# Moving the loads of x, of small tables and of the shared expert at the passage from the woven layers to the mixture

## Chip, cores, metric

One of the eight cores of a Trainium2 chip. The metric is the device time of one execution in microseconds. The kernel reads and writes HBM (device memory); the host only lays arrays out ahead of the launch. In what follows PE is TensorE (matrix products and transposes), DVE is VectorE, ACT is ScalarE, POOL is GpSimd, and SP is SyncE, whose queue issues most of the transfers.

## What is computed

Two layers run on x of 16 samples, each with 256 tokens of width 256, in float32. The first three blocks (two attentions and a quantized feed-forward, with their conditioning) come first; the change lies at the start of the fourth line below.

```python
x = x + attn0(cross_attention(x, fside, braak_embed, itok_B_0_5))
x = x + ffn0(x @ cat_w[itok_B_0_63] + cat_b[itok_B_0_63])
x = x + attn1(diffuse(x, zX, zY, zR))
x = x + ffn1(cond2(x, itok_B_0_15))

def cond2(x, indices):                     # one set of "own" weights for each sample
    h = gelu(x @ fc1_w.T + fc1_b)          # 256 -> 1024, exact gelu
    shared = h @ fc2_w.T + fc2_b           # 1024 -> 192
    own = h @ experts_w[indices].T + experts_b[indices]   # 1024 -> 64
    return concatenate([shared, own], -1)

def ffn1(y):                               # 8 experts, best two, and a shared one
    gates = best_two(softmax(y @ w_router.T))
    acc = gelu(y @ Ws1.T + bs1) @ Ws2.T + bs2
    for e in range(8):
        acc += gates[:, e] * (gelu(y @ W1[e].T + b1[e]) @ W2[e].T + b2[e])
    return acc / sqrt(1.25)
```

## The kernel before

The program has two parts. `woven` runs the first three blocks: nine generators, one for each stage, are merged by a planner with a cost for each instruction, and the order is then written out as it stands. At the end of a sample, its x is written to an HBM tensor of its own, `xd[b]` (L951; shown as L160 by the profile, since the planner records all instructions on that line). The last such write is that of sample 15.

`mixture` (L1034) runs the rest. Its instructions are written in plain order, and a scheduler puts them in order on each engine by what it thinks is ready; each engine then executes its own list in order. SP's list matters here. A transfer issued by SP signals one of eight semaphores, taken in turn, and where a later transfer takes the same semaphore SP first waits until the earlier one has landed. Memory that was used by the woven part comes free with its last users, so that the first load into the tile `xs` waits for the write of `xd[15]`.

`mixture` does this, in source order:

- It loads x of all 16 samples into `xs` (L1046), 256 KiB each.
- It loads small tables: `b1` (L1052), `bs2` (L1053, scaled on DVE by L1054), and in `routing_state` the table `tri` (L1203).
- It loads the shared expert's two matrices, `w1s` and `w2s` (L1058, L1059), 1 MiB each.
- `conditioned` (L1338) loads `fc1` (1 MiB), `fc1b`, `fc2` (the array fc2a, 512 KiB), `fc2b`, `wr` (the router's weights), `expb` (the bias of the own weights, 16x64), and `shared_b`, all by a helper at L1348 or at L1357. It also loads the common part of the own weights (the array fc2c, L1370) into three buffers `own0` to `own2`, which take turns.
- `conditioned` then handles blocks of two samples (512 tokens). For each of the two it loads that sample's own weights (L1377), 128 rows of eight pieces of 256 B. It transposes the block's x on PE (L107, copies at L113 on ACT and DVE into `g_xT`), adds `bs2` to `xs` on POOL (L1387), makes the products with `fc1` (L49, gelu on ACT, L1392), with `fc2` and with `own`, and then transposes the result, multiplies it by the router's weights in the same products with `wr`, and calls `route`. `route` ranks the two best experts, with products of `r_sel` and `seen` on PE, and POOL scatters the rows to the experts' regions in HBM.
- The product of `onehot` with `expb` (L1365) gives a bias for every sample. It stands once, ahead of the blocks.
- After the eight blocks `plan_tiles` assigns expert tiles, four blocks of the shared expert follow (`shared_block`), then the expert tiles, then the other four shared blocks, with the gathering of each token's two rows (`combine`).

Here and in the profile, a line L49 is the helper `mm` for products, and L107 and L113 are the helper `transposed`.

Of the kernel before, what the change touches and what calls it, by code (L numbers as in the profile page):

```python
# [19 lines left out]
P = 128  # L20
# [24 lines left out]
def mm(nc, out, pairs, start=True, stop=True):  # L45

    last = len(pairs) - 1
    for i, (lhsT, rhs) in enumerate(pairs):
        nc.tensor.matmul(out, lhsT, rhs, start=start and i == 0, stop=stop and i == last)  # L49


def bank(k):

    return k.ps.tile([P, 512], F32, name=f"bank{k.stream}", tag=f"bank{k.stream}")


def copies(k):

    k.turn = not k.turn
    return k.nc.scalar.copy if k.turn else k.nc.vector.tensor_copy  # L60
# [973 lines left out]
def mixture(k, out):  # L1034

    nc, tc, a = k.nc, k.tc, k.a
    B, NT = k.B, 2 * k.B
    with ExitStack() as ctx:  # L1040
        k.ps = ctx.enter_context(tc.tile_pool(name="ps", bufs=4, space=bass.MemoryType.PSUM))
        keep = ctx.enter_context(tc.tile_pool(name="moe_keep", bufs=1))

        k.xs = keep.tile([P, NT, D], F32, name="xs")
        for b in range(B):
            nc.sync.dma_start(out=k.xs[:, 2 * b : 2 * b + 2, :], in_=k.xd[b].rearrange("(s p) d -> p s d", p=P))  # L1046
        k.hp = ctx.enter_context(tc.tile_pool(name="moe_h", bufs=2))
        k.p2 = ctx.enter_context(tc.tile_pool(name="moe_p2", bufs=2))
        k.yT = keep.tile([P, 2, B * S], F32, name="yT")
        k.b1 = keep.tile([P, NE + 1, 8], F32, name="b1")  # L1050
        k.bs2 = keep.tile([P, D], F32, name="bs2")
        nc.sync.dma_start(out=k.b1, in_=a["b1"])  # L1052
        nc.sync.dma_start(out=k.bs2, in_=a["b2"][NE : NE + 1].to_broadcast([P, D]))  # L1053
        nc.vector.tensor_scalar(k.bs2, k.bs2, OUT_SCALE, None, ALU.mult)  # L1054
        r = routing_state(k, keep)
        w1s = keep.tile([P, 2, FF1], F32, name="w1s")
        w2s = keep.tile([P, 8, D], F32, name="w2s")
        nc.sync.dma_start(out=w1s, in_=a["w1"][NE])  # L1058
        nc.sync.dma_start(out=w2s, in_=a["w2"][NE])  # L1059
        conditioned(k, keep, r)  # L1060
        k.stream = 1
        plan_tiles(k, keep, r)

        ew = ctx.enter_context(tc.tile_pool(name="moe_w", bufs=2))
        early = 4
        for blk in range(early):
            k.stream = blk % 2
            shared_block(k, r, w1s, w2s, blk)
        expert_tiles(k, ew, r, range(k.n_tiles - SPARE))

        used = nc.values_load(r.used[0:1, 0:1], min_val=0, max_val=k.n_tiles)
        with tc.If(used > k.n_tiles - SPARE):
            expert_tiles(k, ew, r, range(k.n_tiles - SPARE, k.n_tiles))
        for blk in range(early, NT // 4):

            for t in range(4 * (blk - early), 4 * (blk - early) + 4):
                combine(k, r, t, out)
            k.stream = blk % 2
            shared_block(k, r, w1s, w2s, blk)
            for t in range(4 * blk, 4 * blk + 4):  # L1080
                combine(k, r, t, out)


def shared_block(k, r, w1, w2, blk):
# [71 lines left out]
def combine(k, r, t, out):  # L1156

    nc = k.nc
    x = k.xs[:, t, :]
    for i in range(TOPK):  # L1160
        g = k.p2.tile([P, D], F32, name="got", tag="got", bufs=4)
        nc.gpsimd.indirect_dma_start(  # L1162
            out=g,
            out_offset=None,
            in_=k.osort[:, :],
            in_offset=bass.IndirectOffsetOnAxis(ap=r.pos_o[:, i, t : t + 1], axis=0),
        )
        nc.vector.scalar_tensor_tensor(x, g, r.gate[:, i, t : t + 1], x, ALU.mult, ALU.add)  # L1168
    nc.sync.dma_start(out=out[t // 2, (t % 2) * P : (t % 2 + 1) * P, :], in_=x)
# [168 lines left out]
def conditioned(k, keep, r):  # L1338

    nc, tc, a = k.nc, k.tc, k.a  # L1340
    B, NT = k.B, 2 * k.B
    with ExitStack() as ctx:
        w = ctx.enter_context(tc.tile_pool(name="c2_w", bufs=1))
        p2 = ctx.enter_context(tc.tile_pool(name="c2_p2", bufs=2))

        def load(name, shape, src):
            t = w.tile(shape, F32, name=name)
            nc.sync.dma_start(out=t, in_=src)  # L1348
            return t

        fc1 = load("fc1", [P, 2, FF1], a["fc1"])
        fc1b = load("fc1b", [P, 8], a["fc1b"])
        fc2 = load("fc2", [P, 8, P], a["fc2a"])
        fc2b = load("fc2b", [P, 1], a["fc2_b"][0:P].unsqueeze(1))

        wr = w.tile([P, 2, P + NE], F32, name="wr")
        nc.sync.dma_start(out=wr[:, :, P:], in_=a["w_router"])  # L1357
        nc.vector.tensor_copy(wr[:, :, 0:P], k.ident.unsqueeze(1).to_broadcast([P, 2, P]))
        expb = load("expb", [16, 64], a["L1_cond2_experts_b"])

        bias2 = w.tile([P, B], F32, name="bias2")
        shared_b = load("shared_b", [64, 1], a["fc2_b"][P : P + 64].unsqueeze(1))
        nc.vector.tensor_copy(bias2[0:64, :], shared_b.to_broadcast([64, B]))
        pb = bank(k)
        mm(nc, pb[64:128, :B], [(expb, k.onehot[0:16, 2, :])])  # L1365
        nc.vector.tensor_copy(bias2[64:128, :], pb[64:128, :B])
        own = []
        for i in range(3):
            t = w.tile([P, 8, P], F32, name=f"own{i}")
            nc.sync.dma_start(out=t[:, :, 0:64], in_=a["fc2c"])  # L1370
            own.append(t)

        for blk in range(NT // 4):
            k.stream = blk % 2
            for b in (2 * blk, 2 * blk + 1):
                which = nc.sync.value_load(k.idx[0:1, 2, b : b + 1], min_val=0, max_val=15)
                nc.sync.dma_start(  # L1377
                    out=own[b % 3][:, :, 64:128], in_=a["exp_w"][bass.ds(which, 1)].rearrange("e p f m -> p (e f) m")
                )
            xT = p2.tile([P, 2, 512], F32, name="g_xT", tag="g_xT")  # L1380
            transposed(
                k,
                xT.rearrange("p c (s t) -> p (c s) t", t=P),
                [k.xs[:, 4 * blk + s, c * P : (c + 1) * P] for c in range(2) for s in range(4)],
            )
            x = k.xs[:, 4 * blk : 4 * blk + 4, :]
            nc.gpsimd.tensor_tensor(x, x, k.bs2.unsqueeze(1).to_broadcast([P, 4, D]), ALU.add)  # L1387
            hT = k.hp.tile([P, 8, 512], F32, name="hT", tag="hT")
            for f in range(8):
                ph = bank(k)  # L1390
                mm(nc, ph, [(fc1[:, c, f * P : (f + 1) * P], xT[:, c, :]) for c in range(2)])
                nc.scalar.activation(hT[:, f, :], ph, AF.Gelu, bias=fc1b[:, f : f + 1])  # L1392
            py = bank(k)
            mm(nc, py, [(fc2[:, f, :], hT[:, f, :]) for f in range(8)])
            nc.vector.tensor_scalar(k.yT[:, 0, blk * 512 : (blk + 1) * 512], py, fc2b, None, ALU.add)
            for i in range(2):
                b = 2 * blk + i
                py = bank(k)[:, :S]
                mm(nc, py, [(own[b % 3][:, f, :], hT[:, f, i * S : (i + 1) * S]) for f in range(8)])
                nc.vector.tensor_scalar(k.yT[:, 1, b * S : (b + 1) * S], py, bias2[:, b : b + 1], None, ALU.add)  # L1400

            logits = p2.tile([P, 4, NE], F32, name="logits", tag="logits")
            part = p2.tile([P, 4, NE], F32, name="part", tag="part")
            ys = []
            for t4 in range(4):
                tok = slice(blk * 512 + t4 * P, blk * 512 + (t4 + 1) * P)
                py = bank(k)[:, : 2 * (P + NE)].rearrange("p (c w) -> p c w", c=2)
                for c in range(2):
                    mm(nc, py[:, c, :], [(k.yT[:, c, tok], wr[:, c, :])])
                nc.vector.tensor_copy(part[:, t4, :], py[:, 1, P:])  # L1410
                nc.vector.tensor_tensor(logits[:, t4, :], py[:, 0, P:], part[:, t4, :], ALU.add)
                y = p2.tile([P, 2, P], F32, name="r_y", tag="r_y", bufs=5)
                copies(k)(y, py[:, :, 0:P])
                ys.append(y.rearrange("p c d -> p (c d)"))
            route(k, r, p2, logits, ys, 4 * blk, 4)
# [105 lines left out]
```

## Time and profile before

| | |
|---|---|
| median of three runs | 2903.49 us |
| lowest, highest | 2898.98, 2906.39 us |
| the profiled execution | 2904.1 us |
| its span, first to last instruction | 2902.4 us |
| mean granted PE clock | 0.964 |
| PE busy | 2728.9 us, 94% of the span |
| DVE busy | 1437.1 us, 50% |
| ACT busy | 925.0 us, 32% |
| POOL busy | 862.8 us, 30% |
| transfers issued by SP (its queue) | 250.87 MB, 26.9% of 16 transfer engines |

The profile covers one execution, and its times run from the first instruction's start. Busy time is the time in which an engine executes; PE's includes modelled ends of pipelined products. A wait is put down to the event that came last before the waiting instruction began. A transfer is shown at the time at which SP issues it (a row of `SPq`), not at its landing; when it landed is seen from whoever waited for it, and from the rate of the transfer engines in a stretch of time. PEclk is the clock granted to PE, as a share of full speed.

### The profile page before, as it was taken

To read this page: it belongs to the slowest core of one execution; us is meant where nothing else is said; L and a number is where in the kernel's file an instruction comes from. 1 tells how busy PE (TensorE), PEld (TensorE's weight loads), DVE (VectorE), ACT (ScalarE), POOL (GpSimd) and SP (SyncE) were. 2 spreads that over 40 slices of the span, in tenths; PEclk is the share of its full clock that TensorE was granted. 3 is DMA by queue.
4 is the path that set the end of the run, shared out by engine and by line. 5 is a ranking of instruction groups with operands and counts; after the bars stand their busy time and mean duration, and the time that the engine had idled before them with its cause. 6 is when DMAs were issued, how large, how long until landed. Compare 5 with 4: busy or idle time off the path is not lost. (4 is left out here: it accounts for less than half of the span.)

```text
span 2902.4 us, 41871 instructions
## 1 busy us (share of the span) xinstructions
PE 2728.9 (94%) x15819; PEld 2056.7 (71%) x15819; DVE 1437.1 (50%) x3115; ACT 925.0 (32%) x2416; POOL 862.8 (30%) x1030
## 2 busy tenths in 40 slices
PE   5899999999999999999999998869999999999999
PEld 3666667777777777777677767735566788888866
DVE  6566666676676667766776665613332000000023
ACT  2223323333333333333333333313222222222221
POOL 4333333333334334433343333312331000000034
PEclk8799999999899999998999999979999999999999
DMA  3132122222131231231231122141112255555533
GB/s 109 55 95 74 53 90 70 65 93 70 59 99 59 67 101 45 74 108 35 79 104 44 62 88 66 52 144 46 49 48 84 76 190 191 191 193 201 192 100 106
DMA packets 196525, 270.38 MB, mean 93 GB/s; under 512 B 34912, under 2 KB 167264, under 8 KB 186976
## 3 DMA queue, kind: packets, MB, share of 16 engines
q1 hardware_dynamic: 190176, 250.87, 26.9%
q0 software_dynamic: 6144, 16.79, 1.9%
q8 instruction: 127, 2.08, 0.3%
q14 instruction: 78, 0.64, 0.1%
HBM read 207.05 MB, written 60.56 MB: 92 GB/s over the span
## 5 line engine op out<-in xcount | busy, mean ns | idle before, releaser
L160 ACT ACTIVATE f_prob<-pair,f_stat 128x144 f32<-128x144 f32 x512 | 191.1, 378 | 270.1 <-DVE f_stat L160 258.6
L160 DVE TENSOR_TENSOR pair<-pair,mask 128x256 f32<-128x256 f32 (+1 forms) x384 | 197.8, 515 | 123.1 <-PE pair L160 83.2
L160 PE MATMUL single<-e_zT,wq 128*128 128x256 f32 x1024 | 254.0, 392 | 0.0
L49 PE MATMUL bank<-ysT,w 128*128 128x256 f32 x1120 | 247.5, 379 | 0.2 <-ACT ysT L113 0.2
L1162 POOL DMA_INDIRECT got<-osort,pos_o x64 | 62.4, 974 | 623.5 <-PE bank L49 582.5
L49 PE MATMUL bank<-w,ehT 128*128 128x256 f32 x1120 | 247.5, 379 | 0.0
L1144 ACT ACTIVATE ehT<-bank,own_b 128x256 f32<-128x256 f32 x280 | 132.8, 474 | 348.8 <-PE bank L49 348.8
L49 PEld LDWEIGHTS bank<-ysT,w 128*128 128x128 f32 x1120 | 212.7, 190 | 29.4 <-ACT ysT L113 0.5
L49 PEld LDWEIGHTS bank<-w,ehT 128*128 128x128 f32 x1120 | 210.2, 190 | 27.2
L160 PEld LDWEIGHTS single<-e_zT,wq 128*128 128x128 f32 x1024 | 193.4, 196 | 32.8 <-issue 2.8
L160 POOL TENSOR_SCALAR_AFFINE_SELECT b_e<-b_e 128x512 f32<-128x512 f32 x128 | 86.8, 678 | 329.5 <-ACT b_e L160 329.5
L160 PE MATMUL pair<-keys,f_q 32*128 32x144 f32 x2048 | 164.9, 300 | 0.9 <-ACT b_e L160 0.7
L160 PEld LDWEIGHTS pair<-keys,f_q 32*128 32x128 f32 x2048 | 137.2, 190 | 35.9 <-issue 28.0
L160 ACT ACTIVATE b_e<-pair 128x768 f32<-128x768 f32 x128 | 103.7, 811 | 166.2 <-PE pair L160 153.5
L1152 DVE TENSOR_TENSOR eo<-bank,eb 128x512 f32<-128x512 f32 x35 | 24.2, 692 | 234.4 <-PE bank L49 234.4
L160 POOL TENSOR_TENSOR f_q<-f_t,f_t 128x256 f32<-128x256 f32 x128 | 91.8, 736 | 160.7 <-DVE f_t L160 151.3
L160 PE MATMUL single<-wo,f_oT 128*128 128x256 f32 x512 | 129.8, 386 | 9.5 <-ACT f_oT L160 8.4
L160 PE MATMUL pair<-b_qkT 16*128 16x128 f32 (+1 forms) x1024 | 126.9, 371 | 10.9 <-ACT b_qkT L160 7.9
L160 DVE TENSOR_REDUCE qpad<-pair 128x2 f32<-128x256 f32 (+1 forms) x256 | 131.0, 554 | 4.4
L160 DVE TENSOR_TENSOR x<-x,single 128x512 f32<-128x512 f32 (+1 forms) x112 | 68.0, 607 | 128.5 <-PE single L160 127.9
L160 POOL TENSOR_TENSOR keys<-f_t,f_t 128x256 f32<-128x256 f32 x128 | 95.3, 764 | 118.6 <-DVE f_t L160 117.5
L160 PE MATMUL pair<-b_qS,b_qkT 17*128 17x256 f32 (+1 forms) x1024 | 121.7, 357 | 6.2 <-DVE qpad L160 2.8
(290 smaller groups left out, 5235.7 us busy)
## 6 DMA issues: line engine op xcount, KB each, us to landing
w<-in_w SPq DMA_DIRECT2D x70, 1024.0 KB
ysort<-zero SPq DMA_DIRECT2D x32, 1024.0 KB
wq<-in_w_qk SPq DMA_DIRECT2D x128, 256.0 KB
wv<-in_w_v SPq DMA_DIRECT2D x64, 256.0 KB
wo<-in_w_out SPq DMA_DIRECT2D x64, 256.0 KB
ys<-ysort SPq DMA_DIRECT2D x35, 256.0 KB
osort<-eo SPq DMA_DIRECT2D x35, 256.0 KB
eb<-in_b SPq DMA_DIRECT2D x35, 128.0 KB
```

The source lines that it names most:

```text
L49: nc.tensor.matmul(out, lhsT, rhs, start=start and i == 0, stop=stop and i == last)
L160: return Op([(self.name, self.cost(fn, outs, aps), lambda: call(*args, **kw))], outs, aps)
L1144: nc.scalar.activation(hT[:, f, :], ph, AF.Gelu_apprx_tanh, bias=b1[:, f : f + 1])
L1152: nc.vector.tensor_tensor(o, po, b2.unsqueeze(1).to_broadcast([P, 2, D]), ALU.add)
L1162: nc.gpsimd.indirect_dma_start(out=g, out_offset=None, in_=k.osort[:, :], in_offset=bass.IndirectOffsetOnAxis(ap=r.pos_o[:, i, t : t + 1], ...
```

## The change

`load_x` is a new helper for the load of one sample's x. Only the first two samples' x is loaded at the start. In `conditioned`, x of sample b + 2 is loaded after the own weights of sample b. The loads of `w1s` and `w2s` stand after the call of `conditioned` in the source.

```diff
         k.xs = keep.tile([P, NT, D], F32, name="xs")
-        for b in range(B):
-            nc.sync.dma_start(out=k.xs[:, 2 * b : 2 * b + 2, :], in_=k.xd[b].rearrange("(s p) d -> p s d", p=P))
+        for b in range(2):
+            load_x(k, b)
...
+        conditioned(k, keep, r)
         nc.sync.dma_start(out=w1s, in_=a["w1"][NE])
         nc.sync.dma_start(out=w2s, in_=a["w2"][NE])
-        conditioned(k, keep, r)
...
+def load_x(k, b):
+    k.nc.sync.dma_start(out=k.xs[:, 2 * b : 2 * b + 2, :], in_=k.xd[b].rearrange("(s p) d -> p s d", p=P))
...
                     out=own[b % 3][:, :, 64:128], in_=a["exp_w"][bass.ds(which, 1)].rearrange("e p f m -> p (e f) m")
                 )
+                if b + 2 < B:
+                    load_x(k, b + 2)
```

## The prediction

> **What bounds the kernel now.** I read the page's table of busy time first: PE is busy for 94% of the span, the next engine for 50%. A change can pay only where PE stands still. The 40 slices put its one deep dip at 1885 to 1960 us, between the woven layers and the mixture. The waits of PE, asked for 1890 to 2200 us, name what it waits for there. The columns are total us, times, longest.
>
> ```profile
> PE bank L49 <- DMA expb<-in_L_cond_experts_b: 14.9, 1, 14.9
> PE bank L107 <- DMA xs<-xd: 11.6, 1, 11.6
> PE bank L49 <- ACT g_xT L113: 2.7, 6, 0.5
> ```
>
> Two stalls make 26.5 us. Who causes the longer one is read from the timeline of the same stretch (start, length, engine, line, what; in brackets the idle time before it):
>
> ```profile
> 1896.17 0.33 SPq L1348 DMA_DIRECT2D fc<-in_fc  x1
> ...
> 1902.34 9.92 SPq L1046 DMA_DIRECT2D xs<-xd  x16
> ...
> 1907.66 1.99 PE L107 MATMUL bank<-ident,xs 128*128 128x128 f32 x8 [11.62 <-DMA xs<-xd]
> ...
> 1914.90 0.33 SPq L1058 DMA_DIRECT2D w1s<-in_w  x1
> 1915.66 0.33 SPq L1059 DMA_DIRECT2D w2s<-in_w  x1
> ...
> 1917.91 0.45 SPq L1348 DMA_DIRECT2D expb<-in_L_cond_experts_b  x1
> ...
> 1924.59 0.39 PE L49 MATMUL bank<-onehot,expb 16*64 16x16 f32 x2 [14.94 <-DMA expb<-in_L_cond_experts_b]
> ...
> 1926.82 15.42 PE L49 MATMUL bank<-g_xT,fc 128*128 128x512 f32 x32
> ```
>
> expb is 4 KB, but SP issues it after sixteen loads of x (4.2 MB) and both shared matrices (2.1 MB). PE executes in order: everything of block 0 stands behind the little product with expb. The windows show that the transfer engines, not SP, are the brake (after the time: busy PE, PEld, DVE, ACT, POOL, then PEclk, DMA share, GB/s):
>
> ```profile
> 1904.00:1907.00 3.00, 0.00 (x0) 0.00 (x0) 0.00 (x0) 0.00 (x0) 0.00 (x0) 0.50 0.99 313
> 1907.00:1917.00 10.00, 1.99 (x8) 1.43 (x8) 0.00 (x0) 0.00 (x0) 0.00 (x0) 0.50 1.06 341
> 1917.00:1922.00 5.00, 0.00 (x0) 0.00 (x0) 0.29 (x1) 0.00 (x0) 2.34 (x1) 0.50 1.00 406
> 1922.00:1926.00 4.00, 1.41 (x7) 1.38 (x8) 0.93 (x3) 0.00 (x0) 0.00 (x0) 0.50 1.22 216
> ```
>
> The DMA share is full all through: x at some 340 GB/s, the shared matrices at 406 until 1922, then own weights. After 1957 us PE is 99% busy; its waits from 2150 us to the end sum to 2.2 us. Nothing there absorbs an earlier start, and the chain that ended last is PE at its end. So time won at this passage is won at the end.
>
> **What the Trainium skill says.** DMA: Bandwidth & Descriptors, Queues, rings and completion order: each transfer engine consumes the descriptors of a ring in order. The trace agrees: expb, issued at 1917.91, releases PE 6.7 us later, after the shared matrices' stream has ended. The same page, Specifications, puts line rate at pieces of 512 B and more. The trace agrees: own weights, in 256 B pieces, move at 196 to 216 GB/s, x in 1 KB pieces at 341. TensorE: Matmul & The Clock Gate, What's actually happening: after an idle window of about 3.4 us PE runs at half clock, until about as long a busy one; windows run free. The trace agrees: PEclk is 0.50 from 1899 to 1929.6 us, and returns 5.0 us after PE resumes at 1924.59.
>
> **The change, step by step.** The built orders of both kernels differ in three things. SP: after fc1, xd15, fc1b, fc2a come x of samples 0 and 1, b1, bs2, tri, fc2b, wr, expb, shared_b, three own halves (L1370), then own weights of samples 0, 1, 2 with x of 2 and 3 between, x of 4 to 15, w1s and w2s. Only then comes the first own load that waits for PE; so no x stands behind PE, although the source says so. PE: the eight transposes of block 1, done before expb now, follow block 0's last product. ACT and DVE: one copy of block 1 each moves with them. No instruction is added or removed.
>
> *Issue.* SP up to fc2a is unchanged, and the first x load still waits for the write of xd15: 1902.34. The second starts at 1902.76, its successor now at 1903.27 (singled out in the timeline). b1, bs2, tri, fc2b and wr take 0.33 to 0.55 us each: 2.2 us. expb is issued at about 1905.5. In the built order it shares a semaphore with fc2a and must see that landed; now the eighth x load shares it, and starts at 1905.83 at a steady pitch. So 1905.5 to 1905.9.
>
> *Landing.* The x stream starts at 1904.0, 1.6 us after its issue; sample 3's x has passed 1.05 MB later (3.0 us at 341 GB/s) and releases PE at 1908.32, 1.3 us after. expb: 1905.6 + 1.6 + 1.3, and 0.5 for narrow pieces ahead, is 1909.0. Ahead of it are only 0.52 MB of x, gone at 1905.6, and 0.2 MB. The narrow pieces are bounded by the kernel before: 1922.0 to 1924.59, less 1.3, leaves 1.3 us for fc2b, wr and expb together. With none PE starts at 1908.5; with twice that, 1911.1.
>
> *Block 0.* From expb to the first fc1 product took 2.23 us (1924.59 to 1926.82): eight transposes at half clock, a copy on ACT. It is the same again: 1911.2 for 1926.82, a gain of **15.6 us**. The clock should return the same 5.0 us after PE resumes; window phases differ by up to 3.4 us, and half clock costs half: 1.7 us either way.
>
> *Block 1.* Its transposes cost nothing before, as they lay in the stall. Now they cost what block 2's do in the same place: the last product at 1987.44 is followed by 1.04 us of transposes and 0.39 of wait for ACT, to 1988.87. That is **1.4 us lost**. DVE's copy (0.69 us) stands in the route chain, ahead of the rank products; block 2 has the same order and shows no wait at 1994.98. Nothing.
>
> *What else waits.* own0 is needed 22.1 us after the first fc1 product, at 1933.3. Ahead of its landing, and of x for block 1 (needed at about 1942), stand six own halves (1.57 MB at 206 GB/s: 7.6 us) and two x (1.5 us): streamed by 1917, landed by 1918.5. Slack 15 and 23 us. The other x end at 1926 (3.15 MB at 341), the shared matrices at 1931; these are first used at 2175 now, so they cost nothing unless 230 us of cover went. POOL adds bs2 to block 1 later, ahead of block 0's scatters: 2.34 us, done before the positions exist. The three semaphore waits that SP gains before x of 2 and 3 are for fc2b, wr and expb, landed by 1910.
>
> Sum: 15.6 less 1.4 is **14.2 us**. The profiled execution took 2904.1 us (span 2902.4), which gives 2889.9; the median of the runs is 0.6 below it: **2889.5**.
>
> **Rivals.**
> 1. *The stall shrinks less.* One us later at expb is one us less won. The five small loads ahead of it have pieces from 4 to 1024 B, and no row times them alone. If they took 1.3 us each, expb would release PE near 1914.5: 8.7 us won, 2895. Against it: b1, bs2 and tri leave no dip in the 341 GB/s stretch. A relative: the timeline puts ACT's first copy (1926.18) down to the own halves. If that is real, block 0 starts when the third has landed, near 1914: 11 us won, 2892. Against it: in the built order that copy waits only for counts from before the mixture; what the row names is merely the last event, and PE's fourth transpose ended then.
> 2. *No change.* Another input gates block 0. But fc1 and fc2a had landed by 1905.9, since SP passed their semaphores; about 2903.
> 3. *Slower: the clock stays down.* PE resumes with thin work, transposes and a copy between. Each us more at half clock costs 0.5 us. It eats the gain at 28 us of delay, and makes the kernel 8.7 us slower, 2912, at 46. For it: the clock stayed at 0.50 through the transposes of 1907. Against it: those lasted 2 us and a stall followed; the restart at 1924.59 was no denser than the new one.
>
> **How the numbers follow.** 0.3% is 8.7 us, about what a measurement of this kernel can tell from no change. The likeliest case, 0.81, has a gain of 11.5 to 16; rival 1 has 0.13, split about half by the 8.7 us, rival 2 0.03, rival 3 0.03. The shown runs spread from 2899.0 to 2906.4, 3.7 us each way, so some of the likeliest case falls under the bound as well. Faster 0.85, same 0.12, slower 0.03. The range takes 2889.5 with the bounds of landing and clock and that spread: 2884 to 2896.
>
> **What would show it.** In the profile after, PE's wait for expb starts at 1896 and is one wait of about 13 us, ending at 1908.5 to 1911; none on xs before it. SP issues expb near 1905.6, w1s after the last x. The first fc1 product starts near 1911.2, PEclk returns near 1914, block 1's first one comes some 32 us later with 0.4 us of wait for ACT, and no PE wait on own or xs beyond it. A PE wait over 1 us for own weights or for x of block 1, or an fc1 start after 1917, would prove the sum wrong; an fc1 start at 1911 with less than 11 us won at the end would prove the later cover wrong.

## The result and the profile after

The changed kernel takes 2886.68 us (median of 4 runs, 2884.53 to 2889.65) against 2904.94 us (4 runs) for the kernel before: a ratio of 0.994 with an interval from 0.992 to 0.996. A second set of six runs, taken later beside other kernels (e5), gives 2885.94 against 2903.03 us, ratio 0.9939 from 0.9918 to 0.9959. The predicted 2889.5 us is 2.8 us too high, and inside its range. By these intervals the gain lies between some 12 and 24 us; which part of it the change itself brings is read from the traces.

The profiled execution of the kernel after took 2887.37 us, its span is 2885.7 us. These are the waits of PE between 1880 and 2200 us, in the form shown for before (total us, times, longest):

```profile
PE bank L49 <- DMA expb<-in_L_cond_experts_b: 12.2, 1, 12.2
PE single L160 <- POOL f_prob L160: 5.1, 1, 5.1
PE bank L49 <- ACT g_xT L113: 3.2, 7, 0.5
```

Before, two stalls, on xs and on expb, made 26.5 us. Now there is one of 12.2 us, and no wait on xs. The 5.1 us on POOL lie in the woven layers ahead of the passage, and the kernel before has them too. The timeline (start, length, engine, line, what; in brackets the idle time before it) tells how the one stall ends:

```profile
1892.62 0.33 SPq L1352 DMA_DIRECT2D fc<-in_fc  x1
...
1898.79 0.89 SPq L1085 DMA_DIRECT2D xs<-xd  x2
...
1902.24 0.59 SPq L1352 DMA_DIRECT2D expb<-in_L_cond_experts_b  x1
...
1904.70 0.36 PE L49 MATMUL bank<-onehot,expb 16*64 16x16 f32 x2 [12.21 <-DMA expb<-in_L_cond_experts_b]
...
1904.99 1.97 PE L107 MATMUL bank<-ident,xs 128*128 128x128 f32 x8
...
1906.90 15.08 PE L49 MATMUL bank<-g_xT,fc 128*128 128x512 f32 x32
...
1918.40 0.35 SPq L1059 DMA_DIRECT2D w1s<-in_w  x1
```

expb is now issued 3.45 us after the first x instead of 15.6, and w1s comes last. PE has its first fc1 product 14.3 us after SP issued fc1, where it took 30.7. Block 1 follows with the two prices that the prediction put on it, its transposes and one wait for ACT:

```profile
1937.45 1.04 PE L107 MATMUL bank<-ident,xs 128*128 128x128 f32 x8
...
1938.89 6.28 PE L49 MATMUL bank<-g_xT,fc 128*128 128x512 f32 x14 [0.41 <-ACT g_xT L113]
```

The windows of the passage (after the time: busy PE, PEld, DVE, ACT, POOL, then PEclk, DMA share, GB/s) show what became of the load on the transfer engines. They are still busy, though at 161 to 348 GB/s where it was 313 to 406 in these stretches before, and PE now works beside them:

```profile
1904.00:1907.00 3.00, 2.30 (x11) 1.95 (x11) 0.53 (x4) 0.72 (x2) 0.00 (x0) 0.50 0.76 161
1907.00:1917.00 10.00, 10.00 (x21) 4.50 (x22) 0.68 (x1) 4.03 (x6) 2.35 (x1) 0.89 1.19 277
1917.00:1922.00 5.00, 5.00 (x13) 2.27 (x12) 0.00 (x0) 1.93 (x3) 0.00 (x0) 1.00 1.09 348
```

**The account.** The same instructions start at other absolute times from run to run: over the profiled executions of this study SP issues fc1 at 1881.4 (e5) to 1901.4 us (e4), although the program up to there is the same. So every kernel is read from that issue, and called the *passage* is the time from it to the first product with w1s, behind the last of the eight blocks.

| profile | fc1 issued | first fc1 product, after that | first w1s product, after that (passage) | from there to the end of the span |
|---|---|---|---|---|
| before | 1896.17 | 30.65 | 279.07 | 727.1 |
| after | 1892.62 | 14.28 | 263.96 | 729.1 |
| e1 | 1895.92 | 22.34 | 273.1 | 727.1 |
| e2 | 1896.15 | 24.55 | 272.7 | 727.1 |
| e3 | 1896.75 | 13.82 | 266.3 | 727.1 |
| e4 | 1901.40 | 11.12 | 261.1 | 728.8 |
| e5 (after again) | 1881.42 | 14.42 | 264.0 | 728.8 |
| e6 (e4 again) | 1894.46 | 10.96 | 261.0 | 728.8 |

The span fell by 16.7 us: 15.1 at the passage, 3.55 ahead of it, and 1.95 lost again behind it. So the change itself brings 13.2 us. The loss is the one thing that no step of the prediction had; its cause is told with e8 to e12.

The 3.55 us are luck. At 1757 us the two traces lie within 0.1 us of each other. Then, in the kernel before, the clock of PE is at half in two stretches of some 3.4 us in which the kernel after has it whole. Each costs about half of that, 1.7 us. The windows of both kernels there (after the time: busy PE, PEld, DVE, ACT, POOL, then PEclk, DMA share, GB/s), before first:

```profile
1765.00:1770.00 5.00, 5.00 (x26) 3.90 (x24) 0.91 (x3) 1.24 (x6) 0.00 (x0) 0.57 0.01 3
...
1796.00:1801.00 5.00, 5.00 (x29) 4.14 (x28) 2.25 (x5) 2.40 (x10) 1.41 (x2) 0.66 0.00 0
```

```profile
1765.00:1770.00 5.00, 4.32 (x41) 3.44 (x37) 2.60 (x6) 1.77 (x6) 0.31 (x1) 0.92 0.01 3
...
1796.00:1801.00 5.00, 4.31 (x32) 3.43 (x32) 2.71 (x6) 2.75 (x10) 2.40 (x5) 1.00 0.00 0
```

It isn't the change that does this: e8 to e11, which are the kernel after up to block 7, have fc1 issued at 1894.2 to 1898.0 us.

### The profile page after: what moved, and what is told of

It is laid out like the page before. It is cut to its first block, busy times and chain, and to the rows that moved or that the text cites. A ratio compares the mean times of both kernels' runs of the same rounds, so it can differ in the third digit from the quotient of the medians.

```text
span 2885.7 us, 41874 instructions
## 1 busy us (share of the span) xinstructions
PE 2727.3 (95%) x15819; PEld 2054.8 (71%) x15819; DVE 1439.0 (50%) x3115; ACT 925.6 (32%) x2416; POOL 862.8 (30%) x1030
```

## Experiments

**e1 and e2: the two halves of the change.** The theory is that PE starts when expb has landed, and that this is a matter of what SP has issued ahead of it: 2.1 MB of shared matrices and fourteen loads of x. The rival is that one half does everything. e1 is the kernel after with the shared matrices back in their place; e2 is the kernel before with only these moved.

```diff
 e1, against the kernel after
-        conditioned(k, keep, r)
         nc.sync.dma_start(out=w1s, in_=a["w1"][NE])
         nc.sync.dma_start(out=w2s, in_=a["w2"][NE])
+        conditioned(k, keep, r)
 e2, against the kernel before
+        conditioned(k, keep, r)
         nc.sync.dma_start(out=w1s, in_=a["w1"][NE])
         nc.sync.dma_start(out=w2s, in_=a["w2"][NE])
-        conditioned(k, keep, r)
```

> The changed kernel, but with the shared expert's two matrices issued where they were, ahead of fc2b, wr and expb. Measured from the issue of fc1's load to the first product with fc1 (30.65 us before, 14.28 us after the change). Theory (the 4 KB load expb stands in the ring behind whatever is issued ahead of it, and PE stands behind expb): 2.1 MB at 406 GB/s more ahead of expb, so 5.2 us more: 19.5 us, time about 5 us above the changed kernel, 2892. Rival (only the number of x loads ahead counts, the shared matrices do not matter): 14.3 us, time as the changed kernel, 2887.

> The kernel before, with one edit: the shared expert's two matrices are issued last; all sixteen x stay ahead of the tables. Theory (ring order): expb waits for 4.2 MB of x and no longer for 2.1 MB of matrices: 5.2 us less than before, 25.4 us from fc1's issue to its first product; the transposes of block 1 stay in the stall and cost nothing; time about 2899.5. Rival (the matrices alone made the stall): near 14 us, time near 2888.

e1 took 2897.05 us, ratio to before 0.9979 (0.9964 to 0.9993); e2 2897.2 us, 0.9976 (0.9963 to 0.9988). In the traces e1 shortens the passage by 6.0 us, e2 by 6.4, and the whole change by 15.1. Each half leaves PE behind the other half's bytes, so neither alone is the change, and neither is idle. e2 met its number (24.55 us to the first fc1 product, 25.4 expected), though its time came out 2.3 us below the one expected. e1 missed: 22.34 us against 19.5, and a time 5 us above the one expected. Its windows show where to look:

```profile
1904.00:1905.00 1.00, 0.00 (x0) 0.00 (x0) 0.00 (x0) 0.00 (x0) 0.00 (x0) 0.50 0.98 340
1905.00:1907.00 2.00, 0.00 (x0) 0.00 (x0) 0.00 (x0) 0.00 (x0) 0.00 (x0) 0.50 0.69 104
1907.00:1912.00 5.00, 0.00 (x0) 0.00 (x0) 0.29 (x1) 0.00 (x0) 0.00 (x0) 0.50 0.91 367
1912.00:1916.00 4.00, 0.00 (x0) 0.00 (x0) 0.00 (x0) 0.00 (x0) 0.00 (x0) 0.50 0.97 197
```

Between x and the shared matrices the rate falls to 104 GB/s for 2 us, with the transfer engines 0.69 busy; the small loads b1, bs2 and tri stand there in SP's order, issued at 1903.0 to 1904.4. A sum of bytes by the rate of large loads is too small by such a gap. By an estimate from these rates it is worth 1.4 of the 2.8 us missed (2 us at 104 instead of 340 GB/s), and the matrices at 367 instead of 406 GB/s another 0.5. That the small loads make the gap is not shown by a run, and the rest of the miss stays open.

**e3: the 4 KB alone.** The kernel before, all sixteen x and the shared matrices where they were, but with bs2, expb and shared_b loaded ahead of x.

```diff
         k.xs = keep.tile([P, NT, D], F32, name="xs")
+        k.bs2 = keep.tile([P, D], F32, name="bs2")
+        nc.sync.dma_start(out=k.bs2, in_=a["b2"][NE : NE + 1].to_broadcast([P, D]))
+        k.expb = keep.tile([16, 64], F32, name="expb")
+        nc.sync.dma_start(out=k.expb, in_=a["L1_cond2_experts_b"])
+        k.shared_b = keep.tile([64, 1], F32, name="shared_b")
+        nc.sync.dma_start(out=k.shared_b, in_=a["fc2_b"][P : P + 64].unsqueeze(1))
         for b in range(B):
```

> The kernel before, with one edit: expb, shared_b and bs2 (132 KB together) are issued ahead of the sixteen x; x and the shared matrices stay ahead of the own weights. Theory (the place of expb is all): expb is issued 0.5 us after the write of xd15 has landed and PE starts with the transposes of block 0: first product 13.5 to 14.5 us after fc1's issue, as in the changed kernel; PE then meets own0 22 us later, which lands behind 6.3 MB at about 36 us: a wait of 0 to 2 us for own. Time 2887 to 2890. Rival (the x loads of later samples and the matrices have to be moved to win, since own weights or x of block 0 come too late otherwise): a wait of 5 us or more for xs or own, time 2893 or more.

2890.43 us, ratio 0.9949 (0.9936 to 0.9962). The waits of PE in the same stretch as above:

```profile
PE bank L49 <- DMA expb<-in_L_cond_experts_b: 9.5, 1, 9.5
...
PE bank L107 <- DMA xs<-xd: 1.6, 2, 1.0
```

PE has its first fc1 product 13.82 us after fc1's issue, and the passage is 12.8 us shorter than before, of the 15.1 that the whole change brings. So the 4.2 MB of x and the 2.1 MB of shared matrices did little harm as such. What cost most of the time was a small load that had to pass them. (The edit moves 132 KB, most of it bs2; expb is the part that PE waits for.) The other 2.3 us lie behind the first product, which comes 0.5 us earlier than in the kernel after; there this run has waits of PE on DVE, of 1.4 and 0.9 us, that the kernel after doesn't have. No wait of PE on own weights appears, where up to 2 us were expected; in this kernel's order 8 products of block 1 stand ahead of those with own weights. The time is 0.4 us above the range expected.

**e4 and e6: no wait for expb at all.** The kernel after, with the product onehot by expb and the copies around it moved behind block 0's fc1 products. If expb is all that PE waits for, x must be the next to be late, as it lands before expb. e6 is the same kernel beside e5, the kernel after, to compare both on one chip.

```diff
-        nc.vector.tensor_copy(bias2[0:64, :], shared_b.to_broadcast([64, B]))
-        pb = bank(k)
-        mm(nc, pb[64:128, :B], [(expb, k.onehot[0:16, 2, :])])
-        nc.vector.tensor_copy(bias2[64:128, :], pb[64:128, :B])
...
                 nc.scalar.activation(hT[:, f, :], ph, AF.Gelu, bias=fc1b[:, f : f + 1])
+            if blk == 0:
+                nc.vector.tensor_copy(bias2[0:64, :], shared_b.to_broadcast([64, B]))
+                pb = bank(k)
+                mm(nc, pb[64:128, :B], [(expb, k.onehot[0:16, 2, :])])
+                nc.vector.tensor_copy(bias2[64:128, :], pb[64:128, :B])
```

> The changed kernel, with the product of onehot with expb and its two copies made after block 0's products with fc1, so that PE does not wait for expb at the start. Theory (expb is the last to land, x of samples 0 and 1 land some 1.5 us earlier): the wait is for xs, the first product comes 12.6 us after fc1's issue instead of 14.28, time 1.7 us less, about 2885. Rival (expb and x land together, or the ACT copy's many waits set the start): 14 us or more, time as the changed kernel.

> The changed kernel once more, unedited. In its first profile the woven layers ended 3.55 us earlier than before (fc1's load issued at 1892.62 instead of 1896.17) and PE ran 1.9 us longer from the first product with w1s to the end (729.1 instead of 727.2). Theory (both come from the phase of the clock windows in one execution, the change does neither): fc1 is issued anywhere from 1890 to 1902, the last stretch takes 727 or 729; from fc1's issue to its first product 14.3 us, to the first product with w1s 264.0, both within 0.5. Rival (the change does it): 1892.6 within 0.5 and 729.1 again. Time 2884 to 2892.

> The same kernel as e4, beside the changed kernel on one chip. Its passage was 3.2 us shorter by the trace. Theory: 11.1 us from fc1's issue to its first product, 10.4 from the issue of the write of xd15; time 1 to 5 us below the changed kernel. Rival: the gain does not reach the end, time equal within 1 us.

e4 took 2886.52 us, ratio 0.9939 (0.9927 to 0.9951); e6 2885.6 us, 0.9935 (0.9921 to 0.995), beside 2885.94 us of e5. The first fc1 product of e4 came 11.12 us after fc1's issue, earlier than the 12.6 expected: x released PE 3.1 us sooner than expb had in the kernel after, where some 1.5 were thought. PE's wait is now this, in e4:

```profile
PE bank L107 <- DMA xs<-xd: 9.1, 1, 9.1
```

In the traces the passage is 3 us shorter than in the kernel after, in both runs of it (261.1 and 261.0 against 264.0 twice). In the times this is not seen, and e6, which expected 1 to 5 us, met the number of its rival: three us are 0.1%, and the runs of e5 alone spread over 15 us. e5 repeats the passage of the kernel after within 0.15 us. Its fc1 was issued at 1881.4 us, outside the 1890 to 1902 that was expected, which speaks against a fixed gain ahead of the passage. But its last stretch is long again, 728.8 us, so that it left the rival open there.

**e7: what is late next.** x is read from DRAM, where xd15 must have been written, and that write stood behind the 1 MB of fc1: 5.5 us from its issue to the issue of the first x. e7 is e4 with a quarter of fc1 ahead of that write and the rest, with fc2a, b1, bs2 and tri, behind the first two x.

```diff
+        nc.sync.dma_start(out=fc1[:, :, 0 : FF1 // 4], in_=a["fc1"][:, :, 0 : FF1 // 4])
+        with tc.issue_after(k.x1_load.ins):
+            nc.sync.dma_start(out=fc1[:, :, FF1 // 4 :], in_=a["fc1"][:, :, FF1 // 4 :])
...
```

> As e4, and fc1 is loaded in two parts: a quarter (256 KB) ahead of the write of xd15, the rest and fc2, b1, bs2, tri behind x of samples 0 and 1; fc2b, wr, expb and shared_b now fall into SP's wait for xd15. Theory (the write of xd15 lands late, 5.5 us after its issue, because the 1 MB of fc1 stands ahead of it in the ring, and xs waits for it): it lands 3.4 us after its issue, and the first product comes 8.4 us after the issue of that write instead of 10.4 in e4 and 13.6 in the changed kernel; time 2 us below e4. Rival (the write's landing has a fixed length, or the rest of fc1 comes late): the write still takes 5 us, or PE waits over 1 us for the rest of fc1; time as e4 or more.

2886.59 us, ratio 0.9938 (0.9923 to 0.9952). x follows its write by 3.4 us, PE waits 7.4 us for it, and the first fc1 product comes 8.43 us after the issue of the write of xd15 (29.96 in the kernel before, 13.59 after, 10.43 in e4). From the last group of products of the woven layers to the first with w1s it takes 261.0 us, against 261.8 in e4 and 264.7 in the kernel after. Of the 2.0 us won at the start only 0.8 arrive: PE's clock came back 5.9 us after PE resumed, instead of 4.0 in e4, and half of those 1.9 us is most of what is missing. The 2 us that were expected in the time don't show: the median doesn't tell it from e4, so no version of this study is shown to be faster than the kernel after.

**e8 to e12: the loss behind the passage.** The last column of the table has two values: 727.1 us, and 728.8 or 729.1. The difference lies at the If branch behind the expert tiles (L1072 in the kernel before), where PE stands idle for 1.93 to 1.97 us in every kernel. Windows at that place, in the form of above, of the kernel after (PE idle 2766.67 to 2768.61) and of the kernel before (2785.33 to 2787.30):

```profile
2766.50:2768.50 2.00, 0.17 (x1) 0.00 (x0) 0.69 (x1) 0.00 (x0) 0.00 (x0) 1.00 0.12 33
2768.50:2770.50 2.00, 1.89 (x3) 0.83 (x4) 0.00 (x0) 0.00 (x0) 0.00 (x0) 0.69 0.31 105
2770.50:2772.50 2.00, 2.00 (x4) 0.81 (x3) 0.00 (x0) 0.69 (x1) 0.00 (x0) 0.50 0.01 5
2772.50:2774.50 2.00, 2.00 (x6) 0.97 (x5) 0.00 (x0) 0.48 (x1) 1.30 (x2) 0.95 0.00 0
```

```profile
2787.00:2789.00 2.00, 1.70 (x4) 0.87 (x5) 0.00 (x0) 0.00 (x0) 0.00 (x0) 1.00 0.39 132
2789.00:2791.00 2.00, 2.00 (x6) 0.95 (x5) 0.00 (x0) 0.69 (x1) 0.00 (x0) 1.00 0.01 2
```

After the same idle time the clock falls to 0.50 in one kernel and stays at 1.00 in the other. The Trainium skill (TensorE: Matmul & The Clock Gate, What's actually happening) says that the clock is set by the activity in free-running windows of 3413 ns. From this came a theory, made after e1 to e7 were seen: an idle time of 1.95 us lowers the clock if it lies wholly in one window, and does not if a border of the windows cuts it. The return of the clock in the passage is taken as such a border. In the kernel after it lies at 1909.12 us, as the mean of 0.88 in the middle row here tells:

```profile
1908.00:1909.00 1.00, 1.00 (x3) 0.48 (x2) 0.00 (x0) 0.15 (x1) 1.00 (x1) 0.50 1.18 201
1909.00:1909.50 0.50, 0.50 (x2) 0.23 (x2) 0.00 (x0) 0.00 (x0) 0.39 (x1) 0.88 1.29 235
1909.50:1910.00 0.50, 0.50 (x3) 0.26 (x2) 0.00 (x0) 0.00 (x0) 0.00 (x0) 1.00 1.23 249
```

The start of the idle time less that instant, divided by 3.4133 us (the length of a window as closely as the traces give it), gives its place by the part behind the point: 2766.67 less 1909.12 is 251.24 windows, so the place is 0.24. The rival is that the changed order drops the clock for another reason. To tell them apart, one pair of fc1 products of block 7 is issued again, which moves the branch against the windows and changes neither the order of the rest nor the values:

```diff
-                mm(nc, ph, [(fc1[:, c, f * P : (f + 1) * P], xT[:, c, :]) for c in range(2)])
+                for _ in range(3 if blk == NT // 4 - 1 and f == 0 else 1):
+                    mm(nc, ph, [(fc1[:, c, f * P : (f + 1) * P], xT[:, c, :]) for c in range(2)])
```

This is e8; e9 has 5 for the 3, e10 has 2, e11 has 4, and e12 is the kernel before with 2.

> The kernel after, with one pair of fc1 products of block 7 issued three times instead of once: 8 products more on TensorE, about 1.7 us (half of a 3.41 us stretch) between the passage and the If branch; the value is the same, as each repeat overwrites the bank. Theory 'phase': TensorE's clock after the branch depends on where its idle 1.95 us lie in a raster of 3.41 us that runs on from the return of the clock in the passage; in the kernel after they lie at 0.24 to 0.81 of one raster step and the clock falls to half for some 3.5 us; 1.7 us more work moves them to about 0.74 to 1.31, across a border, as in the kernel before, and the clock stays at 1.00. The end from the first product of the shared expert becomes then 728.7 (the kernel after) + 1.7 - 1.6 = about 727 outside the added work: the stretch from the first w1s product to the branch is 1.7 us longer, and the stretch from the branch to the end 1.6 us shorter, so that the span from the first w1s product stays near 728.8. Rival 'the order decides': the clock falls after the branch because of something else in the changed order; then the dip stays and that span is about 730.4.

> The same with the pair issued five times: 16 products more, about 3.4 us, one whole step of the raster. Theory 'phase': the idle time at the branch lies again at about 0.25 to 0.82 of a step, and the clock falls to half after the branch as in the kernel after; the stretch from the branch to the end is as long as in the kernel after. Rival 'more work ahead of the branch lifts the dip in any case': the clock stays at 1.00 as in the shorter addition.

> The kernel after, with one pair of fc1 products of block 7 issued twice instead of once: by the rate of e8_work_half (8 records more in one group, 11.40 against 7.97 us) this is 4 records or 1.72 us of TensorE work more, 0.50 of a step of 3.413 us. Theory 'phase': the idle time at the branch moves from 0.24-0.81 of a step to about 0.74-1.31, across a border; the clock stays at 1.00 after the branch and the stretch from the first w1s product to the end is 727.1 us. Rival 'the changed order lifts or drops the clock': the clock falls after the branch as in the kernel after, and that stretch is 728.7 to 729.1 us.

> The kernel after, with that pair issued four times: 12 records or 5.15 us more, 1.51 steps. Theory 'phase': idle from about 0.75 to 1.32 of a step, no fall of the clock after the branch, 727.1 us from the first w1s product to the end. With e8_work_half and e9_work_full (3.43 and 6.87 us more, 1.0 and 2.0 steps, with the fall) this makes the fall return and go with the step. Rival: the fall is there as in those two, 728.7 to 729.1 us.

> The kernel before, with that pair issued twice: 1.72 us more. Theory 'phase': the idle time moves from 0.67-1.25 of a step to about 1.17-1.75, that is wholly inside one step; the clock, which stays at 1.00 in the kernel before, falls to half for some 3.5 us after the branch, and the stretch from the first w1s product to the end is 728.7 to 729.1 us instead of 727.2. Rival 'the order of the kernel after is what drops it': no fall, 727.2 us.

The sizes of e8 and e9 were wrong by a factor of two: each repeat is four matmul records, not two, so that they added 3.43 and 6.87 us, a whole step and two whole steps of the raster. Both therefore left the idle time where it was, the forecast for e8 was missed, and the fall stayed in both. (Their expectation also put the added work behind the first w1s product; it lies ahead of it, so the last column tells the fall alone.) e10 to e12 have the sizes right.

| profile | added work, us | idle time at the branch, in windows since the clock's return (whole ones left out) | clock after it | first w1s product to end |
|---|---|---|---|---|
| before | 0 | 0.67 to 1.25 | 1.00 | 727.1 |
| e1, e2, e3 | 0 | 0.91 to 1.48, 0.78 to 1.36, 0.91 to 1.49 | 1.00 | 727.1 |
| after, e5 | 0 | 0.24 to 0.81, 0.25 to 0.82 | falls | 729.1, 728.8 |
| e4, e6, e7 | 0 | 0.39 to 0.96, 0.37 to 0.94, 0.12 to 0.68 | falls | 728.7 to 728.8 |
| e8 | 3.43 | 0.24 to 0.81 | falls | 728.8 |
| e9 | 6.87 | 0.24 to 0.81 | falls | 728.8 |
| e10 | 1.72 | 0.76 to 1.33 | 1.00 | 727.1 |
| e11 | 5.15 | 0.76 to 1.33 | 1.00 | 727.1 |
| e12 (before) | 1.72 | 0.14 to 0.72 | falls | 728.8 |

The windows at the branch in e10, where the fall is gone (PE idle 2770.05 to 2772.00), and in e12, where it has come (2784.04 to 2786.00):

```profile
2771.00:2773.00 2.00, 1.00 (x3) 0.55 (x4) 0.00 (x0) 0.00 (x0) 0.00 (x0) 1.00 0.42 137
2773.00:2775.00 2.00, 2.00 (x6) 0.88 (x5) 0.00 (x0) 0.69 (x1) 0.00 (x0) 1.00 0.02 6
```

```profile
2786.00:2788.00 2.00, 2.00 (x4) 1.00 (x5) 0.00 (x0) 0.00 (x0) 0.00 (x0) 0.74 0.26 87
2788.00:2790.00 2.00, 2.00 (x3) 0.76 (x3) 0.00 (x0) 0.69 (x1) 0.53 (x1) 0.50 0.00 0
2790.00:2792.00 2.00, 2.00 (x5) 0.80 (x4) 0.00 (x0) 0.59 (x1) 1.41 (x2) 0.91 0.22 66
```

The fall goes with half a window of added work, returns with one, goes with one and a half, returns with two; and half a window brings it to the kernel before, whose order was never changed. The rival is out. e8 to e12 were run once each (2894.15, 2899.16, 2888.79, 2895.97 and 2904.47 us), so they show this in their traces, not in a median.

The traces hold two more tests of the theory. First, the border needn't be assumed: in all 14 profiles each change of the clock, from the start of the kernel to its end, lies within 0.002 us of a whole number of steps of 3.4133 us from the return in the passage, and the fall at the branch comes 252 to 254 whole steps after it (860.16 us in the kernel after). Second, the woven layers have four idle times of about this length, one of 1.95 us near 1793 us and three of 2.12 us, which no edit touches. In the 14 profiles the clock falls after 23 of these 56, the 23 that lie inside one window, and after none of the 33 that a border cuts. The one near 1793 us is cut in the kernel after and not in the one before: that is the second of the two stretches in the part ahead of the passage.

The place at the branch repeats from run to run, 0.24 and 0.25 in the kernel after and in e5, because the clock returns on a border and the same work follows (from the first w1s product to the branch it takes 610.1 us in every profile). So the loss belongs to the kernel after as it stands, and half a window of added work takes it away.

## Why the prediction was right

*What bounds the kernel* and the main mechanism held: PE stood behind expb, and expb behind bytes of x and the shared matrices. e1, e2 and e3 undo, halve and isolate it, and e4 shows that with the wait gone x is next.

*Issue.* Forecast 9.4 us after fc1's issue (1905.6 less 1896.17), measured 9.62.

*Landing.* Forecast 12.8 us after fc1's issue, measured 12.08. The 1.6 us to the start of the stream, 1.3 to the release and 0.5 for narrow pieces were too much in sum: PE was released 2.46 us after expb's issue.

*Block 0.* From expb to the first fc1 product it took 2.20 us, forecast 2.23. The gain is 30.65 less 14.28, or 16.4 us, for 15.6.

*Block 1.* Its transposes (1.04 us) and its wait for ACT (0.41) came as forecast. The net loss is 1.1 us (31.99 us between the first products of both blocks, for 30.88) and not 1.4, because the clock came back 4.4 us after PE resumed, and 5.1 before (the prediction read 5.0); half of the 0.7 us makes the difference.

*What else waits.* Nothing did in the blocks: no wait of PE on own weights or on x of blocks 1 to 7. w1s was issued at 1918.4 for a use at 2156.6.

*The sum*, 14.2 us at the passage, was 15.1. The total was closer than its parts deserve. The profiled execution came out 2.5 us under the forecast of 2889.9 us: 3.55 us by luck in the part ahead of the passage and 0.9 by the passage itself, less the 1.95 us lost behind it. What the change itself won is 13.2 us, 1.0 less than forecast. The step that failed is the sentence that nothing behind 1957 us absorbs an earlier start, so that time won at the passage is won at the end. It missed the clock: e10 and e11 (727.1 us) against e5, e8 and e9 (728.8) show that 1.7 us of the loss are the fall at the branch. The other 0.3 us appear in no other profile with the fall; 0.24 of them lie at one wait for a gelu of ACT (L1099) at 2814.8 us, and why that came late stays open.

The prediction's reading of the clock was too coarse for this. It took from the page it cites that half clock follows an idle window of about 3.4 us, and called the trace in agreement. But in that trace PE fell idle at 1896.03 us and the clock fell at 1898.99, 2.96 us later, and at the branch 1.95 us of idle time were enough. Here the page and the measurement differ, and the measurement decides: an idle time shorter than a window can lower the clock.

*Rival 1* (the stall shrinks less) had the right kind of worry, a gap by small loads, but it did not occur here; e1 shows one at the place of b1, bs2 and tri. *Rival 2* is refuted by e3, where the place of a few small loads brings 12.8 us. *Rival 3* named the right engine in the wrong place: the clock did come back in the passage, and a price of clock was paid 860 us later: 1.7 us.

## What to carry to other kernels

Look first for the smallest load that an in-order engine waits for, and count what the issuing queue has put ahead of it: moving 132 KB of small loads, 4 KB of them waited for, ahead of 6.3 MB won 12.8 us, and the change that moves the megabytes away brings only 2.3 more. Measure each stage from an event inside the kernel, here an issue on SP, because the same instructions wandered by 20 us between executions while the stage's length repeated within 0.2 us. One or two us can be given back, as at the branch, or be a gift, as ahead of the passage, where a short idle time falls differently against TensorE's clock windows, so read PEclk there before crediting or blaming the edit.

## What the hardware showed that was not expected

An idle time of 1.95 us on PE, a little over half of one window of 3.413 us, lowered the clock for 3.41 us in all eight profiles in which it lay wholly inside one window, counted from the clock's return 860 us earlier, and in none of the six in which a border cut it. It cost 1.7 us each time. The raster holds over a whole execution: all the changes of the clock in 14 profiles lie on it within 0.002 us. This is shown for idle times of 1.93 to 2.14 us only, and the idle share of a window is not the whole rule: 2.12 us that filled 0.57 of one window and 0.05 of the next (near 1433 us in the kernel before) did not lower the clock, while 1.95 us that filled 0.57 of a single one did. Shorter idle times go both ways. In the kernel before, two of 1.5 us lie inside one window each, and the clock fell after the one near 189 us and not after the one near 272 us. In the kernel after, it fell during one of 1.7 us near 1819 us, of which a border cut off the last 0.1 us.

A 4 KB load with little ahead of it released PE 2.46 us after its issue (kernel after) and 2.7 us in e2, where it came behind all of x; in the kernel before, with the shared matrices still streaming at its issue, it took 6.7 us.
